# Largest scores in half blocks, layer statistics on ScalarE, and first and last groups with their own places in the order

## The chip, the cores and the metric

The kernel runs on one NeuronCore of a Trainium2 chip. The metric is the device time of one execution in microseconds (us), the median of several runs of the same program.

## The reference, cut to what matters

One decoder layer works on 64 sequences of 128 tokens with 512 channels. It has three sublayers, each with a layer norm before it and a residual around it:

```python
x = x + ssm(layernorm(x))            # in-projection, causal conv of 4, silu, selective scan
                                     # over 128 tokens with 16 states per channel, gate, out-projection
x = x + attn(layernorm(x), ctx)      # banded attention over the 512 *channels* of a sequence
x = x + moe(layernorm(x))            # 8 experts of width 16, the 2 best per token

# layernorm(x) = (x - mean) / sqrt(var + 1e-5), over the 512 channels of a token
# attn: the roles of tokens and channels are swapped, so there are 512 positions of 128 features,
#       8 heads of 16; position q sees the positions k with |q - k| <= 64
scores = einsum('bqhd,bkhd->bhqk', q, k) / sqrt(16)
scores = where(|q - k| <= 64, scores, most_negative)
attn   = softmax(scores)             # exp(s - max(s)) / sum
```

Two pieces of this are touched: the mean and the variance of each layer norm, and the largest score of each query, which the softmax subtracts.

## The kernel before, in words

The sequences are taken two at a time: 32 groups, each with 256 tokens (`TG`). The work of a group is written as generators ("strands"): `fetch`, `front` (layer norm, transposes, in-projection, conv), `silu0..3`, `project`, `rows_b`, `rows_c`, `dt0`, `dt1` (step sizes), `gate0..3`, `out_proj`, and then for each of the two sequences `attend` and `tail`, and at the end `experts`. The scan over the states is cut into 32 steps for each group (8 blocks of 128 channels, 4 quarters of the states), and each step has the parts `by_b` (GpSimd makes the input h), `decays` (ScalarE makes exp into PSUM), `scan` (VectorE, two halves), `by_c` (VectorE, or `by_c_far` on GpSimd for three steps of eight) and `summed` (TensorE).

The order of all of this is written out by hand and holds for all engines. `PLAN` gives every yield of a strand a place, in steps from the group's first scan step. `STEP` gives each part of a scan step its shift. All items of all groups are sorted by place (lines 910 to 931), and called in that order. So strands of up to five groups are interleaved: while group g is scanned (places 0 to 31), group g+1 goes through `front` to `dt`, group g-1 through `attend` and `tail` (35 to 61), and `experts` of a group comes at 63 to 78. Each engine then works through its own instructions strictly in that order, and waits on semaphores for the others. Since the places are the same for every group, the trace repeats itself from group to group.

Names and lines that matter:

- `moments` (429 to 436): for each of the two sequences, `bn_stats` over 512 channels and `bn_aggr`, on VectorE. It is called three times for each group: at the start of `front` (tile `xf`), after the out-projection (`xr`, called b) and at the start of `experts` (`xr`, called c). `inv_std` (438 to 447) turns the result into scale and bias on GpSimd, and `normalise` (449) applies them on ScalarE.
- `scores` (661 to 676) fills two PSUM tiles `ps_a` (tag "a", two banks each, two buffers in all). First four bf16 matmuls of the identity with the band mask (448 columns), then eight fp32 matmuls of 16 rows (one head at row 32r, four heads side by side), each for a block of 128 queries against 192 or 256 keys. `PAIRS` lists the blocks. `attend` calls it four times for the largest scores (tile `sq`), and VectorE reduces each of the two PSUM tiles with two `tensor_reduce` calls, one for each block (715 to 722). Later `scores` is called again with the roles of queries and keys swapped (tile `sk`), for the exponentials (line 746). That use is not touched.
- The largest scores go through a transposing matmul (`pm`), ScalarE (`nm`) and a small DMA into row 16 of `qT`, where the second scores take them in.
- `take_b` has one PSUM buffer, and serves in-projection, step sizes, transposes, projections of `tail` and `experts`.
- `th` (two buffers in SBUF) is the scratch of `silu`. `dtr`, `dur` (two buffers each) hold the rows of a scan block, `qT`, `kT`, `oT` have one buffer each.

Of the kernel before, what the change touches and what calls it, by code (L numbers as in the profile page):

```python
# [10 lines left out]
BF16 = mybir.dt.bfloat16  # L11
# [6 lines left out]
P = 128  # L18
H = 512
# [24 lines left out]


# [10 lines left out]
        -60.332,  # L56
    ),
    "front": (
        -54.904, -43.416, -41.272, -40.492, -39.654, -38.695, -38.685, -37.888, -36.879,
        -36.408, -36.032, -33.704, -33.145, -32.67, -32.66, -32.343, -31.799, -31.044, -30.174,  # L60
        -28.281, -27.454, -26.855, -26.832,
    ),
    "silu0": (
        -24.781, -24.46, -24.257,
    ),
    "silu1": (
        -29.838, -26.427, -25.073,
    ),
    "silu2": (
        -27.027, -26.806, -24.454,  # L70
    ),
    "silu3": (
        -22.5, -22.354, -21.641,
    ),
    "project": (
        -21.132, -21.099, -20.786, -19.777,
    ),
    "rows_b": (
        -11.803, -11.114, -2.288, -1.642,
    ),  # L80
    "rows_c": (
        -6.008, -5.135, -0.454, -0.226,
    ),
    "dt0": (
        -19.146, -19.123, -18.828, -18.586, -18.576, -18.517, -18.507, -18.497, -16.555,
        -16.496, -16.464, -16.226, -15.68, -14.582, -13.949, -11.966, -9.752,
    ),
    "dt1": (
        -8.54, -8.53, -7.168, -6.931, -4.396, -3.985, -3.344, -2.893, -2.009, -0.644, -0.166,
        1.263, 3.073, 6.784, 6.958, 7.293, 9.75,  # L90
    ),
    "gate0": (
        -5.443, 3.125, 3.277, 3.457,
    ),
    "gate1": (
        6.075, 6.704, 6.947, 6.957,
    ),
    "gate2": (
        11.935, 13.43, 13.746, 14.883,
    ),  # L100
    "gate3": (
        17.102, 18.411, 19.344, 19.54,
    ),
    "out_proj": (
        14.098, 15.108, 25.166, 27.955, 28.249, 28.897, 31.185, 31.344, 33.251, 34.471, 34.878,
        35.042,
    ),
    "attend0": (
        35.319, 35.465, 35.633, 36.089, 36.766, 37.24, 37.729, 37.739, 38.09, 38.1, 38.319,
        38.329, 38.606, 38.616, 38.847, 38.915, 38.925, 39.077, 39.333, 39.384, 39.646, 39.769,  # L110
        39.874, 40.107, 40.224, 40.234, 40.244, 40.509, 40.621, 41.595, 41.894, 42.165, 42.565,
        42.575, 42.887, 42.954, 42.964,
    ),
    "tail0": (
        41.092, 43.917, 43.927, 44.704, 45.578, 45.841, 45.851, 47.675, 48.362, 48.641, 49.437,
        49.792,
    ),
    "attend1": (
        43.598, 44.297, 44.545, 44.882, 44.892, 45.231, 45.409, 45.569, 45.741, 46.002, 46.012,
        46.644, 46.9, 46.991, 47.295, 47.744, 47.933, 47.943, 48.059, 48.685, 48.695, 49.273,  # L120
        49.283, 50.058, 50.791, 50.801, 51.134, 51.424, 51.549, 51.851, 51.861, 52.706, 52.72,
        53.308, 53.741, 53.751, 54.874,
    ),
    "tail1": (
        49.808, 55.232, 56.972, 57.846, 59.014, 59.685, 59.961, 60.274, 60.284, 60.387, 61.028,
        61.206,
    ),
    "experts": (
        62.814, 64.883, 65.122, 65.98, 66.07, 66.08, 66.253, 66.772, 67.628, 67.64, 69.657,
        69.884, 70.093, 70.31, 70.406, 71.21, 72.072, 72.112, 72.932, 73.648, 73.928, 78.062,  # L130
# [3 lines left out]
STEP = {  # L134
    "loads": (-3.6, 0, 0, 0, -3.754, 0, 0, 0),
    "by_b": (-0.407, -0.939, -0.855, -0.458, -0.757, -0.972, -1.605, -1.622),
    "decays.0": (-0.306, -0.611, -0.011, -0.125, -0.644, -0.63, -0.649, -0.336),
    "scan.0": (0, 0.29, 0.673, 0.224, -0.426, -0.43, -0.079, 0.045),
    "by_c.0": (0, 0.685, 0.811, 0, -0.425, -0.117, 0, 0.212),
    "decays.1": (0.032, -0.305, 0.297, 0.193, -0.488, -0.409, -0.309, -0.213),  # L140
# [854 lines left out]
```

## Time and profile before

| | |
|---|---|
| runs of the kernel | 5680.31, 5680.67, 5683.51 us (median 5680.67) |
| the profiled execution's own time | 5693.28 us |
| its span, first to last instruction | 5691.6 us |
| TensorE matmul busy | 4854.9 us (85%) |
| VectorE busy | 4729.5 us (83%) |
| GpSimd busy | 4562.8 us (80%) |
| ScalarE busy | 3701.2 us (65%) |
| first scan starts, last scan starts | 135.5 us, 5537.8 us |
| mean granted TensorE clock | 0.921 |

"Busy" is the time in which the engine has an instruction in work; matmuls are pipelined, and their ends are modelled. The lines of the page name the source line (L719 is line 719), the engine, the operation, and the tiles "out<-in" with partitions x elements. PE is TensorE, PEld its weight loads, DVE VectorE, ACT ScalarE, POOL GpSimd, SP the engine that issues the DMAs. A matmul of fp32 leaves two records in the trace, one of bf16 leaves one. The chain of waits follows the program back from its last instruction, at each step to what released it.

In the middle of the run the start of every 64th scan, one for each group, lies 170.1 us after the last one (mean over the groups 3 to 28). The first group takes 150.5 us.

### The profile page before, as it was taken

What the parts mean: (1) busy time and instruction counts of PE and PEld (TensorE: products, weight loads), DVE (VectorE), ACT (ScalarE), POOL (GpSimd) and SP (SyncE); (2) the same over time, 40 slices, a digit from 0 to 9 for tenths busy, and PEclk for the clock granted to TensorE, in tenths of its full rate; (3) what the DMA queues carried; (4) which work ended last, traced back from release to release, by engine and by line L of the source; (5) the groups of instructions that cost most, each with busy time, mean ns of one, the idle gap of its engine ahead of it and who ended that gap; (6) DMA issues with size and microseconds to landing.
All of it is one profiled execution on the core that took longest, in us unless ns stands there. A gap on an engine that the chain in (4) does not pass through costs nothing.

```text
span 5691.6 us, 91135 instructions
## 1 busy us (share of the span) xinstructions
PE 4854.9 (85%) x33348; PEld 2698.4 (47%) x33348; DVE 4729.5 (83%) x6896; ACT 3701.2 (65%) x7138; POOL 4562.8 (80%) x2818
## 2 busy tenths in 40 slices
PE   4689888889888889888889888889888888888886
PEld 3345445445445445545445445445444444444432
DVE  2788888888888888888888888888888888888882
ACT  2566767666767666667666667676666676666752
POOL 4888888888888788888888888888888888888860
PEclk7899999999999999999999999999999999999887
DMA  2333333333333333333333333333333333333320
GB/s 79 118 112 110 125 114 129 121 115 107 125 117 126 122 114 113 119 117 127 124 112 116 118 116 125 131 108 117 121 109 129 127 120 108 118 119 115 120 87 20
DMA packets 282192, 650.00 MB, mean 114 GB/s; under 512 B 48912, under 2 KB 116496, under 8 KB 281744
## 3 DMA queue, kind: packets, MB, share of 16 engines
q1 hardware_dynamic: 281744, 644.18, 33.3%
q8 instruction: 262, 4.29, 0.3%
q14 instruction: 186, 1.52, 0.1%
HBM read 557.04 MB, written 85.98 MB: 113 GB/s over the span
## 4 chain that ended last, share of the span: by engine, by line
PE 52%; DVE 19%; ACT 18%; issue 4%; DMA 4%; POOL 3%; SPq 0%; DVEq 0%; POOLq 0%; ACTq 0%
PE pin L463 9%; DVE mx L719 7%; ACT da L366 6%; PE yp L407 5%; PE pg L463 5%; PE sk L671 4%; PE po L644 4%; PE sq L671 3%; DVE hc L385 3%; PE pw L793 3%; ACT pe L746 3%; DVE u L512 3%; PE sk L665 3%; PE pa L753 2%; PE sq L665 2%
## 5 line engine op out<-in xcount | busy, mean ns | idle before, releaser
L354 POOL TENSOR_TENSOR h<-dur,brep 128x1024 f32<-128x1024 f32 x1024 | 2423.1, 2375 | 217.1 <-DVE da L385 171.2
L366 ACT ACTIVATE da<-dtr,acol 128x256 f32<-128x256 f32 x4096 | 1923.2, 476 | 837.7 <-DVE hc L385 398.6
L385 DVE TENSOR_TENSOR_SCAN da<-da,h 128x512 f32<-128x512 f32 x1280 | 1542.2, 1219 | 171.5 <-ACT da L366 135.2
L395 POOL TENSOR_TENSOR hc<-hc,crep 128x1024 f32<-128x1024 f32 x384 | 905.6, 2358 | 574.7 <-DVE hc L385 544.2
L385 DVE TENSOR_TENSOR_SCAN hc<-da,h 128x512 f32<-128x512 f32 x768 | 912.8, 1213 | 169.9 <-ACT da L366 83.3
L390 DVE TENSOR_TENSOR hc<-da,crep 128x512 f32<-128x512 f32 x1280 | 855.3, 685 | 59.2 <-PE yp L407 14.5
L407 PE MATMUL yp<-hc,sely 128*32 128x256 f32 x8192 | 754.5, 431 | 52.9 <-POOL hc L395 40.0
L719 DVE TENSOR_REDUCE mx<-sq 128x2 f32<-128x512 f32 (+1 forms) x1024 | 570.9, 614 | 175.7 <-PE sq L671 175.7
L746 ACT ACTIVATE pe<-sk 128x896 f32<-128x896 f32 x512 | 445.0, 915 | 137.9 <-PE sk L671 135.3
L463 PE MATMUL pin<-xnT,wi 128*128 128x256 f32 x2048 | 515.5, 408 | 21.4 <-DVE u L512 7.5
L463 PE MATMUL pg<-xnT,wi 128*128 128x256 f32 x2048 | 489.7, 393 | 8.1 <-DVE u L512 5.0
L644 PE MATMUL po<-wo,y 128*128 128x512 f32 x1024 | 470.2, 602 | 0.5 <-DVE y L415 0.5
L463 PEld LDWEIGHTS pin<-xnT,wi 128*128 128x128 f32 x2048 | 407.6, 204 | 129.5 <-ACT brep L566 23.7
L512 DVE SCALAR_TENSOR_TENSOR u<-pin,cw,u 128x254 f32<-128x254 f32 (+2 forms) x768 | 309.1, 471 | 164.5 <-ACT u L504 164.3
L463 PEld LDWEIGHTS pg<-xnT,wi 128*128 128x128 f32 x2048 | 388.2, 195 | 110.3 <-ACT dt L589 15.6
L665 PE MATMUL sq<-mask,identb 128*128 128x448 bf16 x1024 | 289.8, 384 | 159.2 <-DVE mx L719 154.8
L665 PEld LDWEIGHTS <-identb 128*128 128x128 bf16 x2048 | 162.0, 100 | 526.6 <-DVE mx L719 288.2
L407 PEld LDWEIGHTS yp<-hc,sely 128*32 128x32 f32 x8192 | 203.6, 114 | 404.6 <-issue 201.9
L671 PE MATMUL sk<-qT,kT 32*128 32x192 f32 (+1 forms) x4096 | 272.3, 381 | 45.6 <-DMA qT<-nm 45.6
L671 PE MATMUL sq<-kT,qT 16*128 16x192 f32 (+1 forms) x4096 | 300.6, 413 | 0.0
L644 PEld LDWEIGHTS po<-wo,y 128*128 128x128 f32 x1024 | 193.7, 192 | 222.4 <-issue 217.9
L665 PE MATMUL sk<-mask,identb 128*128 128x448 bf16 x1024 | 265.4, 373 | 28.6 <-ACT pe L746 21.6
(149 smaller groups left out, 6739.6 us busy)
## 6 DMA issues: line engine op xcount, KB each, us to landing
wi<-in_w_inproj SPq DMA_DIRECT2D x256, 512.0 KB
dtr<-dtd SPq DMA_DIRECT2D x256, 512.0 KB
dur<-dud SPq DMA_DIRECT2D x256, 512.0 KB
wo<-in_w_outproj SPq DMA_DIRECT2D x128, 512.0 KB
dtd<-dt SPq DMA_DIRECT2D x256, 128.0 KB
dud<-e SPq DMA_DIRECT2D x256, 128.0 KB
rc<-rd SPq DMA_DIRECT2D x256, 128.0 KB
xf<-in_x SPq DMA_DIRECT2D x64, 256.0 KB
```

Of the source, the lines that this page charges most:

```text
L354: nc.gpsimd.tensor_tensor(hs[k], dur[g, ib], brep[g, j // 2][:, j % 2, :].unsqueeze(1).to_broadcast([P, 4, TG]), ALU.mult,)
L366: nc.scalar.activation(das[k, half][:, s, :], dtr[g, ib][:, c, :], AF.Exp, scale=acol[:, col : col + 1])
L385: nc.vector.tensor_tensor_scan(flat(to), flat(d), flat(hs[k][:, own, :]), 0.0, ALU.mult, ALU.add)
L390: nc.vector.tensor_tensor(product(k)[:, 2 * half : 2 * half + 2, :], das.pop((k, half)), c_rows(k, 2), ALU.mult)
L395: nc.gpsimd.tensor_tensor(hcs[k], hcs[k], c_rows(k, 4), ALU.mult)
L407: nc.tensor.matmul(yps[g, ib][32 * c : 32 * c + 32, :], sely, h[:, c, :], start=False, stop=(j == NJ - 1), skip_group_check=True,)
L463: nc.tensor.matmul(ps[:, s * TG : (s + 1) * TG], w[:, s, k, :], flat3(xnT[g][:, k, :, :]), start=(k == 0), stop=(k == HC - 1),)
L644: nc.tensor.matmul(po[:, b, :], y[g, c][:, b * P : (b + 1) * P], w[:, c - c2, :], start=(c == 0), stop=(c == IC - 1),)
L665: nc.tensor.matmul(ps[r // 2][:, r % 2, :PAIR], identb, mask[:, i * EDGE : i * EDGE + PAIR], start=True, stop=False,)
L671: nc.tensor.matmul(ps[r // 2][:, r % 2, c0 : c0 + r1 - r0], left[32 * r : 32 * r + rows, s, blk * P : (blk + 1) * P], right[32 * r : 32 * ...
L719: nc.vector.tensor_reduce(mx[:, blk, h0 : h0 + 2], ps[rp][:, :, c0 : c0 + r1 - r0], AX.X, ALU.max,)
L746: nc.scalar.activation(t, ps[rp][:, :, :PAIR], AF.Exp, scale=0.25)
```

## The change

1. A new function `largest` takes the place of `scores` for the largest scores. It works in half blocks of 64 queries. Every half block sees exactly 192 keys (`WIN`), from `first_key`. Where `scores` had eight matmuls of 128 queries with 192 or 256 keys, `largest` has sixteen of 64 queries with 192 keys: four heads side by side in the rows, and two halves (queries 0 to 63 and 64 to 127 of a block) side by side in the columns. A new mask `maskq` of 3 x 192 columns is built at the start, and the mask matmuls have 384 columns. VectorE reduces each PSUM tile with one `tensor_reduce` of 768 elements, with four results for each partition, in place of two of 512 and 384.
2. `moments` goes to ScalarE: for each sequence one ACTIVATE Identity with scale -1/512 whose accumulator gives minus the mean, and one ACTIVATE Square with that as its bias, whose accumulator gives the sum of squares. Its scratch tile `sq` shares the tag `th`. `inv_std` scales the sum by 1/512. After the residual add of the out-projection a yield is added, so that `moments` b has its own place.
3. All places in `PLAN` and `STEP` are new. The first group has its own places for `front` to `dt`, the last group for `out_proj` to `experts`. In the last sequence of all, `qT` and `kT` lie in buffers of `dtr` and `oT` in one of `dur`.

The program has 4096 fp32 matmuls of 64 queries for these scores in place of 2048 of 128, 512 reduces for 1024, no `bn_stats` or `bn_aggr` (384 instructions less), and 384 more ACTIVATEs. The number of activation table loads is the same, 129, and the number of DMAs too. The orders on the engines have the same pieces between the same neighbours for most of a group. ScalarE has `moments` b behind the copy `xfT` of the first sequence and ahead of the copy `plv`, `moments` c behind the conv start `u` of the second in-projection, and `moments` a ahead of the relu of `pw`. For the first group, the two `pbrep` products come ahead of and behind `pts`, and the statistics of group 1 ahead of the step sizes of group 0. At the end, the 21 small VectorE operations of the experts of group 30 stand ahead of the reduces of group 31, and not among them.

The diff without the tables of places:

```diff
+WIN = 3 * LOCAL
 PLAN = {
...
+def first_key(q0):
+    return min(max(q0 - LOCAL, 0), H - WIN)
...
+    nc.gpsimd.memset(maskf[:, : 3 * WIN], 0.0)
+    for c, q0s in enumerate(((0, LOCAL), (P, P + LOCAL), (H - P, H - LOCAL))):
+        for q0 in q0s:
+            off = first_key(q0) - q0
+            m = maskf[q0 % P : q0 % P + LOCAL, c * WIN : (c + 1) * WIN]
+            select(m, ALU.is_ge, LOCAL + off, [[1, WIN]], -1, NEG)
+            select(m, ALU.is_ge, LOCAL - off, [[-1, WIN]], 1, NEG)
+    maskq = fixed([P, 3 * WIN], "maskq", dtype=BF16)
+    nc.vector.tensor_copy(maskq, maskf[:, : 3 * WIN])
...
     def moments(src, name):
-        mv = work([P, GB, 2], "mv", 3, f"mv_{name}")
-        st = [work([P, 6], "st", 4, f"st_{name}_{b}") for b in range(GB)]
-        for b in range(GB):
-            nc.vector.bn_stats(st[b], src[:, b, :])
-        for b in range(GB):
-            nc.vector.bn_aggr(mv[:, b, :], st[b])
+        mv = work([P, 2, GB], "mv", 3, f"mv_{name}")
+        sq = work([P, H], "th", 2, f"sq_{name}")
+        for b in range(GB):
+            nc.scalar.activation(
+                sq, src[:, b, :], AF.Identity, scale=-1.0 / H, accum_out=mv[:, 0, b : b + 1]
+            )
+        for b in range(GB):
+            nc.scalar.activation(
+                sq, src[:, b, :], AF.Square, bias=mv[:, 0, b : b + 1],
+                accum_out=mv[:, 1, b : b + 1],
+            )
         return mv
...
-        nc.gpsimd.tensor_scalar(rs[:, 0, :], mv[:, :, 1], EPS, None, ALU.add)
+        nc.gpsimd.tensor_scalar(rs[:, 0, :], mv[:, 1, :], 1.0 / H, EPS, ALU.mult, ALU.add)
...
         nc.vector.tensor_tensor(flat(t), flat(po), flat(t), ALU.add)
+        yield
         mv = moments(t, f"b{g}")
...
+    def largest(q, k, s, i, name):
+        ps = [take_a(f"{name}_{s}_{i}_{rp}") for rp in range(2)]
+        for r in range(4):
+            nc.tensor.matmul(
+                ps[r // 2][:, r % 2, : 2 * WIN], identb, maskq[:, i * WIN : (i + 2) * WIN],
+                start=True, stop=False, skip_group_check=True,
+            )
+        for half in range(4):
+            q0 = (4 * i + half) * LOCAL
+            k0 = first_key(q0)
+            for r in range(4):
+                nc.tensor.matmul(
+                    ps[r // 2][
+                        q0 % P : q0 % P + LOCAL, r % 2, half // 2 * WIN : (half // 2 + 1) * WIN
+                    ],
+                    q[32 * r : 32 * r + HD, s, q0 : q0 + LOCAL],
+                    k[32 * r : 32 * r + HD, s, k0 : k0 + WIN],
+                    start=False, stop=(half == 3), skip_group_check=True,
+                )
+        return ps
...
     def attend(g, b):
+        far = g == n_groups - 1 and b == 1
...
-                ps = scores(qT, kT, HD, s, i, f"sq_{n}")
+                ps = largest(qT, kT, s, i, f"sq_{n}")
                 for rp in range(2):
                     yield
-                    for blk, c0, r0, r1 in PAIRS[i]:
-                        h0 = 4 * s + 2 * rp
-                        nc.vector.tensor_reduce(
-                            mx[:, blk, h0 : h0 + 2], ps[rp][:, :, c0 : c0 + r1 - r0],
-                            AX.X, ALU.max,
-                        )
+                    h0 = 4 * s + 2 * rp
+                    nc.vector.tensor_reduce(
+                        mx[:, 2 * i : 2 * i + 2, h0 : h0 + 2].rearrange("p k h -> p h k"),
+                        ps[rp][:, :, : 2 * WIN].rearrange("p h (k j) -> p h k j", j=WIN),
+                        AX.X, ALU.max,
+                    )
...
+    def own(g, name):
+        if g == 0 and name.startswith(("front", "silu", "project", "rows", "dt")):
+            return "_first"
+        if g == n_groups - 1 and name.startswith(("out_proj", "attend", "tail", "experts")):
+            return "_last"
+        return ""
...
-            for p in PLAN[name]:
+            for p in PLAN[name + own(g, name)]:
```

## The prediction, made before the run

> **What bounds the kernel now.** I read the page first, then the repeating stretch in the middle, then the waits of each engine, and last the single operations that the change touches.
>
> ```profile
> PE 4854.9 (85%) x33348; PEld 2698.4 (47%) x33348; DVE 4729.5 (83%) x6896; ACT 3701.2 (65%) x7138; POOL 4562.8 (80%) x2818
> PE 52%; DVE 19%; ACT 18%; issue 4%; DMA 4%; POOL 3%; SPq 0%; DVEq 0%; POOLq 0%; ACTq 0%
> ```
>
> Three engines are nearly equally full. The chain runs mostly over PE, a fifth each over DVE and ACT. Busy time by windows of one group each:
>
> ```profile
> 2007.00:2177.00 170.00, 149.59 (x1045) 82.62 (x1043) 147.65 (x216) 115.63 (x225) 142.11 (x87) 0.93 0.35 119
> sum 510.00, PE 447.64 PEld 248.68 DVE 441.50 ACT 345.50 POOL 424.90; mean PE 149.21 PEld 82.89 DVE 147.17 ACT 115.17 POOL 141.63
> ```
>
> A group takes 170.1 us (spacing of the first scans), and PE, DVE and POOL work 149, 147 and 142 of it. Each stands still for 21 to 28 us, so nobody is a clean bound. The waits of the whole run say who waits for whom:
>
> ```profile
> POOL hc L395 <- DVE hc L385: 544.2, 233, 11.7
> ACT da L366 <- DVE hc L385: 398.6, 196, 9.2
> DVE mx L719 <- PE sq L671: 175.7, 131, 12.9
> PE sq L665 <- DVE mx L719: 154.8, 227, 2.3
> DVE da L385 <- ACT da L366: 135.2, 210, 1.7
> ```
>
> POOL and ACT wait for DVE. PE waits for DVE at the largest scores, and DVE for PE there. That place, `sq` and `mx`, is where the change cuts. In the chain of the stretch 2007 to 2177 it looks like this, and nearly all eight score tiles of a group lie on it:
>
> ```profile
> 2076.22 0.76 PE sq L665 x4
> 2076.98 0.98 PE sq L671 x16
> 2077.98 2.22 DVE mx L719 x4
> ```
>
> **Part 1, the reduces.** Groups by shape:
>
> ```profile
> L719 DVE TENSOR_REDUCE mx<-sq 128x2 f32<-128x512 f32 x512 | 348.7, 681 | 94.7 <-PE sq L671 94.7
> L719 DVE TENSOR_REDUCE mx<-sq 128x2 f32<-128x384 f32 x512 | 280.5, 548 | 81.0 <-PE sq L671 81.0
> L433 DVE BATCH_NORM_STATS2 st_b<-xr 128x6 f32<-128x512 f32 x64 | 41.2, 686 | 1.1
> L435 DVE BATCH_NORM_AGGREGATE mv_b<-st_b 128x2 f32<-128x6 f32 x64 | 9.6, 173 | 0.0
> L549 ACT ACTIVATE th<-u 128x512 f32<-128x512 f32 x128 | 79.7, 623 | 4.6 <-POOL u L553 2.6 <-DVE u L512 2.0
> L450 ACT ACTIVATE xf<-xf,rs_a 128x512 f32<-128x512 f32 x64 | 48.1, 799 | 19.4 <-POOL rs_a L444 19.4
> ```
>
> 128 more elements cost 681 - 548 = 133 ns, so 1.04 ns each above 149 ns. One reduce of 768 should take 149 + 768 x 1.04 = 948 ns. A group has 16 x 681 + 16 x 548 = 19.7 us of reduces now, and 16 x 948 = 15.2 us after: 4.5 us less DVE work. On the chain a run of four takes 2.14 to 2.23 us (overlapping by 0.09 at each seam), and two would take 2 x 0.948 - 0.09 = 1.80, so 0.38 less. From 1000 to 5082 us the chain has L719 on it with 7.3%, 12.4 us of a group or 5.7 such runs. That gives **-2.1 us**.
>
> **Part 2, the score matmuls.** Mask matmuls follow each other by 189 ns for 448 columns, so 162 for 384. On the chain they have 3.7 us of a group, and a seventh of that is **-0.5 us**. The fp32 part isn't in the trace in its new form. Now four heads run side by side in the rows, in four passes one after the other (two for 192 keys at 162 ns, two for 256 at 216, the first 0.27 because it loads its weights in the open): 0.27 + 0.16 + 0.22 + 0.22 = 0.86 us. After, there are eight passes of 162 ns for each head. If the two column halves ran fully side by side it would be four passes, 0.27 + 3 x 0.16 = 0.75 us. If they ran one after the other, eight, 1.40 us. If an instruction only has to wait for its own half, the passes overlap like a chain of five: 0.27 + 4 x 0.16 = 0.92. I take 0.92, for this reason. The Trainium skill ("TensorE: Matmul & The Clock Gate", section "Part 3: Packing small matmuls — row/col tiling") says that a weight load overlaps running matmuls only when it goes to other rows of the array. By that rule the halves, which share their rows, queue up, with weight loads in the open too: 8 x (0.16 + 0.13), where 0.13 is between the 106 ns load of 32 columns and the 185 of 128. That is 2.3 us, 12 us more for a group. But this trace has four column tiles that share all rows:
>
> ```profile
> 2077.88 0.64 PE L407 MATMUL yp<-hc,sely 128*32 128x256 f32 x8
> ```
>
> Eight records of 256 columns in 0.64 us, where alone each takes 216 ns: they do overlap, weight loads included (these start 7 ns apart). So the row decides against the rule, and PE's load stays about where it is: (0.92 - 0.86 - 4 x 0.027) x 8 = -0.4 us, from -1.7 to +3.5 by the rows, +11 by the rule. On the chain: **0**.
>
> **Part 3, the statistics.** 6 x 0.68 + 6 x 0.173 = 5.1 us of DVE work go. They are hardly on the chain, but scans queue behind them. Outside the reduces, DVE's 127 us a group have 19 on the chain, 15%: **-0.8 us**. ACT gets two ACTIVATEs without a pointer operand (like L549, 0.62) and two with one (between 0.62 and 0.80), three times a group. With 0.09 overlap and a short wait for its own mean, that is 2.5 us each time, 7.5 a group. The accumulator's price is not in the trace: at least nothing (7 us a group), at most a second small instruction for each (12 x 0.22 us, L846), without overlaps 12 us. I take 7.5, by the row it is nearest to. The skill's "ScalarE: Activation LUTs" (section "Rules for kernel authors") says to leave adds and multiplies to VectorE; as a sum over both engines it is right here (7.5 for 5.1 us), but ACT is 68% full and DVE 87%. What is behind these ACTIVATEs on ACT are `decays`, and DVE's scans wait for those. By the order, `moments` b stands where DVE has two scans and two products ahead (3.8 us), c where it has two scans and six conv operations (4.8 us), a ahead of the relu of `pw`. All are longer than 2.5 us, so they mostly hide: **+0.6 us**. If that cover were gone all 7.5 would show. The extra latency of b and c (2.5 against 1.7) goes into strands with places to spare. POOL keeps its operations, SP its DMAs, and table loads stay at 129.
>
> **Part 4, the places.** In the middle the order has the same pieces between the same neighbours. I give the new places nothing; they may be worth 2 us either way.
>
> Sum for a group: -2.1 - 0.5 - 0.8 + 0.6 = -2.8 us; 31 spacings: -87 us. **The ends.** Before the first scan lie 135.5 us. Group 0's step sizes get two products, two copies and the statistics of group 1 ahead of them, but the first scan waits on ACT for the conv start of group 1 (132.07), itself behind a weight DMA and two in-projections, that is kept. I put +2. Building `maskq` costs POOL 0.6 + 12 x 0.36 = 4.9 us where it is idle for 35.6 us. After the last scan lie 153.8 us: seven runs of reduces, -2.7; statistics b and c, +2.2; the 21 small operations of the experts, which stood between two runs of reduces for 4.0 us, now run while PE makes q and k, -4. The buffers for the last `qT`, `kT`, `oT` free little: the chain there is one of data. Ends together -3. So 5693.3 - 87 - 3 = 5603 for the profiled execution; it lay 12.6 us above the median of 5680.7, so **5591, I say 5590**.
>
> **The rivals.**
> (a) DVE paces everything. For: most waits of POOL and ACT end on it. Against: half of the chain is PE's own work. Then the 9.6 us that DVE loses come back nearly whole, 8 a group: 5681 - 31 x 8 = 5430. Chance 0.12.
> (b) PE is the bound: its 149 us stay, the shorter reduces only turn PE's waits for `mx` into waits for something else (`pt` for ACT's step sizes has 229 us already), and ACT's extra work eats the rest. Also what would follow if an accumulator cost much. 5680, within 11 us. Chance 0.10.
> (c) Slower: the column halves of `largest` do not overlap. Place: between mask and reduce, on the chain. Price: 0.54 - 0.11 = 0.43 us x 8 = +3.4 us a group with hidden weight loads, against the -2.3 of the reduces, statistics and ScalarE: 5680 + 31 x 1.2 = 5717; with weight loads in the open, 5980. I put 5730, nearer the first, since loads overlap in every row here. It decides from 1.15 us for the sixteen matmuls, where its extra eats those 2.3. The loss would also come if all of `moments` lay open, +7.5 - 0.6 a group, 5804. Chance 0.25 together.
> The likeliest (d), DVE's savings on the chain and half hidden otherwise: 0.53.
>
> **How the numbers follow.** Two tenths of a per cent, 11 us, is about what a measurement can tell from no change. (d) alone runs from 5540 to 5645: the places at 2 us a group either way make 62 us, the score matmuls between -0.8 and 0 on the chain 25. To leave no more than 2 in 10 out, the range takes in (b), half of (c), and the upper part of (a): 5500 to 5725. Faster: 0.53 + 0.12 = 0.65; same 0.10; slower 0.25.
>
> **What would show it.** Right: the spacing of first scans near 167.3; reduces near 950 ns; a sixteen-matmul block near 0.92 us; PE's 149 unchanged, DVE near 138, ACT near 123. Wrong: score blocks of 1.4 us or more; ACT rows with accumulator above 0.9 us; DVE's wait for `da` (135 us in the run) doubled; PE's waits grown by what `mx` gave back.

## The result, and the profile after

The changed kernel takes 5699.83 us (median of 7 runs, 5693.75 to 5711.18), the kernel before 5681.42 us beside it (7 runs). The ratio is 1.0031, 95% interval 1.0020 to 1.0043: slower by a third of a per cent, inside the stated range, but slower where faster was forecast. The profiled execution of the changed kernel took 5698.44 us, its span is 5696.3 us. The mean clock granted to TensorE was 0.904 to 0.909 in the seven runs; in the timed runs of the kernel before it lay between 0.915 and 0.924.

The shares of the span and the chain of waits:

```profile
PE 4828.3 (85%) x37444; PEld 2725.5 (48%) x37444; DVE 4544.7 (80%) x6001; ACT 3977.4 (70%) x7906; POOL 4577.8 (80%) x2831
PE 49%; ACT 20%; DVE 17%; issue 4%; DMA 4%; POOL 3%; SPq 1%; DVEq 0%; ACTq 0%; POOLq 0%
```

Busy time in the windows of the middle (columns as before: PE, PEld, DVE, ACT, POOL, clock, DMA):

```profile
2007.00:2177.00 170.00, 148.29 (x1170) 84.13 (x1169) 141.01 (x188) 123.37 (x247) 141.60 (x87) 0.92 0.35 118
sum 510.00, PE 444.89 PEld 252.45 DVE 423.40 ACT 370.03 POOL 424.74; mean PE 148.30 PEld 84.15 DVE 141.13 ACT 123.34 POOL 141.58
```

DVE lost 6.0 us a group of busy time (8.8 us as a sum of durations), ACT gained 8.2, PE lost 0.9, at a clock of 0.92 where it was 0.93. Yet the spacing of the first scans (groups 3 to 28) is 170.4 us, where it was 170.1: DVE is relieved, and the period doesn't move. The rest lies at the start: the first scan begins at 138.4 us, 2.9 later; after the last scan comes 153.2 us, 0.6 less.

The waits of the whole run:

```profile
DVE hc L467 <- ACT da L448: 196.4, 151, 3.1
...
DVE da L467 <- ACT da L448: 119.3, 168, 2.4
...
DVE mx L834 <- PE sq L780: 80.4, 63, 5.3
```

DVE waits 95 us less for the scores. Its waits for the decays (`da`) went from 219 to 316 us, and it has waits that it did not have before, shown below. Single operations, by shape:

```profile
L834 DVE TENSOR_REDUCE mx<-sq 128x4 f32<-128x768 f32 x512 | 464.3, 948 | 80.8 <-PE sq L780 80.4
L780 PE MATMUL sq<-kT,qT 16*64 16x192 f32 x8192 | 274.4, 383 | 0.0
L520 ACT ACTIVATE sq_b<-xr,mv_b 128x512 f32<-128x512 f32 x64 | 46.2, 722 | 2.1
L516 ACT ACTIVATE sq_b<-xr 128x512 f32<-128x512 f32 x64 | 40.4, 632 | 3.4 <-DVE xr L740 2.4
L516 ACT ACTIVATION_READ_ACCUMULATOR sq_b<-xr 128x1 f32 x64 | 12.2, 190 | 0.0
```

The reduce takes the 948 ns that were worked out. The score matmuls are as cheap as taken where the clock is full, and take 1.7 times as long where it is halved (shown under part 2 below). Each accumulator costs an instruction of its own, which the program does not name.

### The profile page after: what moved, and what is told of

The parts are those of the page before. It is cut to its first block, busy times and chain, and to the rows that moved or that the text cites. A ratio compares the mean times of both kernels' runs of the same rounds, so it can differ in the third digit from the quotient of the medians.

```text
span 5696.3 us, 99361 instructions
## 1 busy us (share of the span) xinstructions
PE 4828.3 (85%) x37444; PEld 2725.5 (48%) x37444; DVE 4544.7 (80%) x6001; ACT 3977.4 (70%) x7906; POOL 4577.8 (80%) x2831
## 4 chain that ended last, share of the span: by engine, by line
PE 49%; ACT 20%; DVE 17%; issue 4%; DMA 4%; POOL 3%; SPq 1%; DVEq 0%; ACTq 0%; POOLq 0%
PE pin L551 8%; ACT da L448 6%; PE po L732 6%; PE yp L489 5%; ACT pe L866 5%; DVE mx L834 4%; PE sk L760 4%; PE pg L551 4%; DVE da L467 3%; PE pw L913 3%; DVE hc L467 3%; PE sk L754 2%; PE sq L780 2%; PE pa L873 2%; PE pqk L799 2%
## 5 line engine op out<-in xcount | busy, mean ns | idle before, releaser
L472 DVE TENSOR_TENSOR hc<-da,crep 128x512 f32<-128x512 f32 x1280 | 869.8, 688 | 75.3 <-PE yp L489 19.9
L489 PE MATMUL yp<-hc,sely 128*32 128x256 f32 x8192 | 737.8, 420 | 83.0 <-POOL hc L477 65.4
L834 DVE TENSOR_REDUCE mx<-sq 128x4 f32<-128x768 f32 x512 | 464.3, 948 | 80.8 <-PE sq L780 80.4
L551 PE MATMUL pin<-xnT,wi 128*128 128x256 f32 x2048 | 495.5, 397 | 31.6 <-DVE xr L924 12.8
L551 PEld LDWEIGHTS pin<-xnT,wi 128*128 128x128 f32 x2048 | 395.0, 198 | 137.4 <-ACT crep L654 36.0
L772 PE MATMUL sq<-maskq,identb 128*128 128x384 bf16 x1024 | 274.3, 377 | 128.8 <-DVE mx L834 121.9
L754 PE MATMUL sk<-mask,identb 128*128 128x448 bf16 x1024 | 288.9, 383 | 71.1 <-ACT pe L866 34.8
L780 PE MATMUL sq<-kT,qT 16*64 16x192 f32 x8192 | 274.4, 383 | 0.0
L760 PEld LDWEIGHTS sk<-qT,kT 32*128 32x128 f32 x4096 | 189.7, 200 | 156.7 <-DMA qT<-nm 81.1
```

The costliest lines, as they stand in the source:

```text
L472: nc.vector.tensor_tensor(product(k)[:, 2 * half : 2 * half + 2, :], das.pop((k, half)), c_rows(k, 2), ALU.mult)
L489: nc.tensor.matmul(yps[g, ib][32 * c : 32 * c + 32, :], sely, h[:, c, :], start=False, stop=(j == NJ - 1), skip_group_check=True,)
L551: nc.tensor.matmul(ps[:, s * TG : (s + 1) * TG], w[:, s, k, :], flat3(xnT[g][:, k, :, :]), start=(k == 0), stop=(k == HC - 1),)
L754: nc.tensor.matmul(ps[r // 2][:, r % 2, :PAIR], identb, mask[:, i * EDGE : i * EDGE + PAIR], start=True, stop=False,)
L760: nc.tensor.matmul(ps[r // 2][:, r % 2, c0 : c0 + r1 - r0], left[32 * r : 32 * r + rows, s, blk * P : (blk + 1) * P], right[32 * r : 32 * ...
L834: nc.vector.tensor_reduce(mx[:, 2 * i : 2 * i + 2, h0 : h0 + 2].rearrange("p k h -> p h k"), ps[rp][:, :, : 2 * WIN].rearrange("p h (k j) ...
```

## The experiments

Two theories stood against each other. Theory 1: the statistics cost far more on ScalarE than the 0.6 us taken for them. Theory 2: the new places cost, which were given nothing. (In the expectations below, S is theory 1 and P is theory 2; W says that what is saved turns into waits wherever it is saved.) The three parts of the change can be separated, so the first six experiments fill a table of operations by places. "Old places" means the tables `PLAN` and `STEP` of the kernel before (and no yield ahead of `moments` b). All were timed beside the kernel before, whose median was 5682.58 to 5695.57 us from one timing to the next, so ratios are compared. "A group" is the spacing of the first scans, as above.

**1. The largest scores alone, old places.**

```diff
-            nc.scalar.activation(
-                sq, src[:, b, :], AF.Identity, scale=-1.0 / H, accum_out=mv[:, 0, b : b + 1]
-            )
...
+            nc.vector.bn_stats(st[b], src[:, b, :])
+        for b in range(GB):
+            nc.vector.bn_aggr(mv[:, b, :], st[b])
...
-    "loads": (-2.237, 0, 0, 0, -4.054, 0, 0, 0),
+    "loads": (-3.6, 0, 0, 0, -3.754, 0, 0, 0),
...
```

> The kernel before with the half-block largest scores alone; statistics stay on VectorE, all places are the old ones. Theory P (the operations give what the prediction summed, and the new places lose it again): 2.6 us less a group, 5681 - 31 x 2.6 = 5600 us. Theory W (the reduces' saving turns into waits wherever it is put, because the engines wait for each other in a ring): 5681 within 20 us. Theory S (the statistics on ScalarE lose what the reduces gain): 5600 us, as P.

Measured 5578.18 us, ratio 0.9795 (0.9779 to 0.9812), spacing 166.6 us. Parts 1 and 2 of the prediction, the reduces and the score matmuls, bring 2 %, more than the whole forecast.

**2. The statistics alone, old places** (`scores` and `PAIRS` reduces for the largest scores as before).

```diff
-                ps = largest(qT, kT, s, i, f"sq_{n}")
+                ps = scores(qT, kT, HD, s, i, f"sq_{n}")
```

> The kernel before with the statistics on ScalarE alone, old places. P: the statistics are nearly free, +0.6 - 0.8 us a group, 5681 within 25 us. W: 5681 within 25 us too, since ScalarE has idle time. S: each of the three pieces of 3.3 us (two ACTIVATEs of 0.63, two of 0.72, four reads of the accumulator of 0.19, less overlap) holds up the decays behind it and with them the scans, about 3 us a group, 5775 us.

Measured 5883.29 us, 1.0332 (1.0306 to 1.0358). This is 6 us a group (176.1 against 170.1), twice what theory 1 expected.

**3. Both, old places.** The changed kernel with the tables of before:

```diff
-        yield
         mv = moments(t, f"b{g}")
...
-    "loads": (-2.237, 0, 0, 0, -4.054, 0, 0, 0),
+    "loads": (-3.6, 0, 0, 0, -3.754, 0, 0, 0),
...
```

> The kernel before with both operations changed and all places old. P: 5590 us, the prediction's own sum, since it gave the new places nothing. W: 5681 within 25 us. S: 5600 + 95 = 5695 us, about what the changed kernel takes.

Measured 5786.98 us, 1.0162 (1.0144 to 1.0181), spacing 173.3.

**4. The new places alone**: the changed kernel with the scores and the statistics of before.

```diff
-                ps = largest(qT, kT, s, i, f"sq_{n}")
+                ps = scores(qT, kT, HD, s, i, f"sq_{n}")
...
+            nc.vector.bn_stats(st[b], src[:, b, :])
...
```

> The changed kernel with the old operations put back (scores of 128 queries with two reduces, statistics on VectorE): only the places are new. P: the new places alone cost what the operations gain, 5681 + 110 = 5790 us. W: 5681 to 5720 us. S: the new places are neutral, 5681 within 30 us.

Measured 5814.65 us, 1.0209 (1.0192 to 1.0226), spacing 174.1.

**5. The largest scores with the new places**, statistics on VectorE (the second edit of experiment 4 alone).

> The changed kernel with the statistics back on VectorE; half-block scores and new places stay. So far: half-block scores alone 0.9795, statistics on ScalarE alone 1.0332, both 1.0162, new places alone 1.0209. Theory S (the statistics on ScalarE are the loss in any order): about as much faster than the changed kernel as in the old order, 5700 - 200 = 5500 us. Theory O (order and operations belong together: the new places were made for statistics on ScalarE, and there they cost little): 5690 to 5720 us, the sum of the new places' own loss (+119) and the reduces' gain (-117).

Measured 5698.43 us, 1.0030 (1.0019 to 1.0040), spacing 170.7.

**6. The statistics with the new places**, scores as before (the first edit of experiment 4 alone).

> The changed kernel with the old scores and two reduces; statistics on ScalarE and new places stay. S: new places +119 and statistics +188 add up, 5990 us. O: the statistics cost little or nothing in the order that has room for them, 5815 us or less (the changed kernel 5700 and the reduces' 117).

Measured 5749.30 us, 1.0117 (1.0104 to 1.0131). The table, as ratios to the kernel before:

| | old places | new places |
|---|---|---|
| scores of before, statistics on VectorE | 1 | 1.0209 |
| largest, statistics on VectorE | 0.9795 | 1.0030 |
| scores of before, statistics on ScalarE | 1.0332 | 1.0117 |
| both | 1.0162 | 1.0031 (the change) |

Both theories hold, and they are tied to each other. Read down: `largest` gains in every pair (2.05, 1.70, 1.79 and 0.86 %). The statistics cost 3.3 and 3.7 % at the old places, and gain 0.9 % or nothing at the new. Read across: the new places cost 2.1 and 2.4 % where the statistics are on VectorE, and give back 2.2 and 1.3 % where they are on ScalarE. The new order fits the moved statistics, and costs elsewhere about as much as `largest` brings. How much of each of these differences goes with the granted clock is looked at behind experiment 17.

**7. The ends.** The changed kernel without the own places of the first and the last group, and without the other buffers of the last sequence:

```diff
-            for p in PLAN[name + own(g, name)]:
+            for p in PLAN[name]:
...
-        far = g == n_groups - 1 and b == 1
+        far = False
```

> The changed kernel without places of their own for the first and last group: all groups use the general places, and the last sequence the usual buffers. If the own places help at the ends: up to 20 us slower than the changed kernel, 5720 us. The spans of the ends (135.5 and 153.8 us before, 138.4 and 153.2 us after) say that they do little: 5700 us within 8 us.

Measured 5698.27 us, 1.0028 (1.0017 to 1.0039): the ends make no difference that can be told.

**8. Occupancy or latency.** Experiment 1, and ScalarE makes its passes too, into tiles that nobody reads; the statistics used are VectorE's. So ScalarE's time is added, nothing waits for its results, and VectorE keeps its work.

```diff
         for b in range(GB):
             nc.vector.bn_aggr(mv[:, b, :], st[b])
+        dv = work([P, 2, GB], "dv", 3, f"dv_{name}")
+        sq = work([P, H], "th", 2, f"sq_{name}")
+        for b in range(GB):
+            nc.scalar.activation(
+                sq, src[:, b, :], AF.Identity, scale=-1.0 / H, accum_out=dv[:, 0, b : b + 1]
+            )
...
         return mv
```

> The half-block scores with old places (5578 us) and statistics on VectorE, whose values are used. In addition ScalarE makes the same twelve passes with accumulators at the same places of its queue, and nobody reads their results. So ScalarE is as full as with the statistics on it, but no chain hangs on it. If it is ScalarE's occupancy that holds up decays and scans: as slow as both operations together, 5787 us, or a little over, since VectorE keeps its 5.1 us a group (5800 to 5850). If it is the chain of accumulator, GpSimd and normalise, with GpSimd's queue held at the scale (127 us of waits in the run with statistics alone): near 5578 us, at most 5620.

Measured 5755.15 us, 1.0127 (1.0113 to 1.0140). Of the 3.7 % between experiments 1 and 3, 3.3 come from ScalarE's time alone. The later result matters little, and so does what VectorE is spared.

**9. One place changed.** From the trace I worked out how long ScalarE has nothing in work between the starts of scan step k and k+1 of a group (experiment 1, mean of twelve groups). It is 51 us in all, but 0.2 us in each of the steps 2 and 3, where b stands at the old places, 0.6 and 0.2 in the steps 8 and 9, where a stands, 6.0 in step 31, where c stands, and 10.3 in step 6. In experiment 3 just the steps 1 to 3 are longer (by 3.0 us together) and 8 and 9 (by 3.5), and 31 is not. So a was moved from step 9 to step 6, in experiment 3:

```diff
     "front": (
-        -54.904, -43.416, -41.272, -40.492, -39.654, -38.695, -38.685, -37.888, -36.879,
+        -57.6, -43.416, -41.272, -40.492, -39.654, -38.695, -38.685, -37.888, -36.879,
```

> Both operations with the old places (5787 us), and one number changed: the statistics a, 3.3 us on ScalarE, move from step 9 of the scan to step 6. In the run with half-block scores alone ScalarE stands still for 10.3 us of step 6, and for 0.2 us of step 9. Theory I (a piece costs in full where ScalarE has no idle time in that step, and nothing where it has): the 3.5 us a group that the run with both operations lost around step 9 come back, 5787 - 31 x 3.5 = 5680 us. If the mere load of ScalarE counts, 5787 within 15 us.

Measured 5691.07 us, 1.0012 (1.0004 to 1.0020). One number takes off 1.5 %. Step 9 is back from 7.75 to 4.95 us, and step 6 grows no longer (13.96 and 13.94 us, means of 25 groups), while ScalarE's idle time in it falls from 10.6 to 7.6.

**10. a (moved) and c on ScalarE, b on VectorE**, largest scores, old places. The edit of experiment 9, and

```diff
     def moments(src, name):
+        return (moments_s if name[0] in "ac" else moments_d)(src, name)
```

> Half-block scores, old places, statistics a (moved to step 6) and c (step 31, 6.0 us of idle ScalarE) on ScalarE, b back on VectorE. I: nothing lost against half-block scores alone (5578 us), and the 3.4 us of VectorE work a group that go save up to 2 us a group: 5520 to 5578, say 5560 us. If the load of ScalarE counts: two thirds of the 177 us that twelve passes with unread results cost, 5690 us.

Measured 5606.66 us, 0.9857 (0.9844 to 0.9871). A miss: this was to beat experiment 1, and is 0.5 to 0.6 % slower. VectorE is spared 3.4 us a group and nothing comes of it.

**11 and 12. Which table costs?** Experiment 5 (largest, new places) with the old `STEP`, and experiment 1 (largest, old places) with the new `STEP`.

```diff
-    "by_b": (-0.434, 0.126, -0.462, -0.28, -0.571, -1.445, -1.504, -1.889),
+    "by_b": (-0.407, -0.939, -0.855, -0.458, -0.757, -0.972, -1.605, -1.622),
...
```

The diff is that of experiment 11; 12 has it the other way round.

> Half-block scores and statistics on VectorE with the new places of the strands, but the old shifts of the scan's parts. The same operations take 5578 us in the old order and 5698 in the new one. If the strands carry that loss: 5690 us. If the shifts of the scan do: 5590 us. If both only fit together: over 5700 us.

> Half-block scores and statistics on VectorE with the old places of the strands and the new shifts of the scan's parts. If the strands carry the loss of the new order: 5590 us. If the shifts do: 5690 us. If both only fit together: over 5700 us.

Measured 6026.71 us, 1.0594 (1.0579 to 1.0608), and 6027.33 us, 1.0600 (1.0585 to 1.0614). Inconclusive: each half of the new order is far worse with the old other half. The tables belong together, so swapping one of them does not tell which holds the cost.

**13 to 16. One piece at a time**, all on experiment 1: b alone on ScalarE, c alone, a alone at its old place, a alone at the earlier place. (`moments_s` is the changed function, `moments_d` that of before.)

```diff
     def moments(src, name):
+        return (moments_s if name[0] in "b" else moments_d)(src, name)
```

> The largest scores in half blocks at the old places (5578 us), with statistics b alone on ScalarE. Theory A (a piece costs what ScalarE's idle time in its step doesn't cover; at the steps 2 and 3 ScalarE has 0.2 us idle each): +3.0 us a group, 31 x 3.0 = 93, so 5670 us. Theory B (the three pieces together overfill ScalarE, and one alone is absorbed by its 51 us of idle time in a group): within 12 us of 5578.

> The same with statistics c alone on ScalarE, at step 31, where ScalarE has 6.0 us idle. Theory A: +0.2 us a group, 5584 us. Theory B: within 12 us of 5578 too. If c is what made the version with a (moved) and c 28 us slower, it is about 5600.

> The same with statistics a alone on ScalarE, at its old place (step 9, where ScalarE has 0.2 us idle, and 0.6 in the step before). Theory A: +3.5 us a group, 5687 us. Theory B: within 12 us of 5578.

> The same with statistics a alone on ScalarE, at the earlier place (step 6, 10.3 us idle). Theory A: 0 to +0.5 us a group, 5578 to 5594 us, so about 96 us below the run with a at its old place. Theory B: no difference between the two places of a.

Measured: b 5691.38 us, 1.0012 (1.0003 to 1.0021); c 5595.71, 0.9844 (0.9830 to 0.9857); a 5654.34, 0.9946 (0.9933 to 0.9958); a moved 5585.11, 0.9824 (0.9811 to 0.9838). Against 0.9795 that is +2.2, +0.5, +1.5 and +0.3 %. The pieces add up: 2.2 + 0.5 + 1.5 = 4.2 % for the 3.7 that they cost together. One piece alone is not absorbed by 51 us of idle time elsewhere in the group; it decides where it stands. In size the account by steps was off both ways, if the ratios are turned into us a group: b cost 4.0, not 3.0, a 2.8 and not 3.5 (a gives 0.8 us back in the steps 6 and 8, b loses 1.2 more there), c 0.9 and not 0.2. For b and c most of this goes with the clock, as shown behind experiment 17.

Piece b in experiment 13. ScalarE's timeline (start, time, what):

```profile
2169.27 0.99 ACT L385 ACTIVATE da<-dtr,acol 128x256 f32<-128x256 f32 x2
2170.20 0.61 ACT L473 ACTIVATE sq_b<-xr 128x512 f32<-128x512 f32 x1
...
2173.26 0.80 ACT L501 ACTIVATE xn<-xr,rs_c 128x512 f32<-128x512 f32 x1
2173.97 0.97 ACT L385 ACTIVATE da<-dtr,acol 128x256 f32<-128x256 f32 x2
```

VectorE's beside it:

```profile
2170.30 1.23 DVE L404 TENSOR_TENSOR_SCAN da<-da,h 128x512 f32<-128x512 f32 x1 [0.87 <-ACT da L385]
2171.57 0.69 DVE L409 TENSOR_TENSOR hc<-da,crep 128x512 f32<-128x512 f32 x1
2175.02 1.22 DVE L404 TENSOR_TENSOR_SCAN hc<-da,h 128x512 f32<-128x512 f32 x1 [2.77 <-ACT da L385]
```

The piece takes 3.1 us (2170.20 to 2173.26), between the decays of one scan and those of the next. VectorE has one scan and one product left, 1.9 us, and then stands for 2.8 us. In experiment 1 the same scans follow each other without it:

```profile
2131.89 1.22 DVE L404 TENSOR_TENSOR_SCAN da<-da,h 128x512 f32<-128x512 f32 x1
2133.14 0.69 DVE L409 TENSOR_TENSOR hc<-da,crep 128x512 f32<-128x512 f32 x1
2133.75 1.21 DVE L404 TENSOR_TENSOR_SCAN hc<-da,h 128x512 f32<-128x512 f32 x1
```

At the new places the cover is there. In the changed kernel ScalarE has b behind the decays of two more scans:

```profile
2163.67 1.89 ACT L448 ACTIVATE da<-dtr,acol 128x256 f32<-128x256 f32 x4
2167.02 0.58 ACT L942 COPY xfT<-ptc 128x512 f32<-128x512 f32 x1 [1.47 <-PE ptc L544]
2167.51 0.63 ACT L516 ACTIVATE sq_b<-xr 128x512 f32<-128x512 f32 x1
...
2170.74 1.90 ACT L448 ACTIVATE da<-dtr,acol 128x256 f32<-128x256 f32 x4
```

and VectorE works through them:

```profile
2169.19 1.22 DVE L467 TENSOR_TENSOR_SCAN da<-da,h 128x512 f32<-128x512 f32 x1
...
2171.82 2.34 DVE L467 TENSOR_TENSOR_SCAN hc<-da,h 128x512 f32<-128x512 f32 x2 [0.68 <-POOL rs_b L530]
2176.21 0.69 DVE L712 SCALAR_TENSOR_TENSOR gt<-gt,pg 128x512 f32<-128x512 f32 x1 [2.05 <-ACT gt L710]
```

ScalarE's idle time at this place is 3.4 us in experiment 5, which has the new order and nothing to fill it, and 0.1 us in the changed kernel. The new order holds a gap open for the piece. The last line shows a wait that came with that order: VectorE stands for the tanh of the gate. In the stretch from 1000 to 5082 us, by group, experiment 5 has these waits of VectorE that experiment 1 lacks: 2.3 us for that tanh, 1.7 for the products of the step sizes on GpSimd, 1.0 for their exp, 0.9 for a row of sums from a DMA, and 3.5 more for decays ahead of the `hc` scans; its wait for the score matmuls falls from 4.8 to 0.3.

**17. One such wait taken out**, in the changed kernel. The product stands ahead of a scan whose decays are ready:

```diff
     "gate0": (
-        -5.691, 2.931, 3.333, 3.625,
+        -5.691, 2.931, 3.333, 4.0,
```

> The changed kernel with one number of its places changed: the product of the first gate on VectorE, at 3.625 just ahead of the first scan of step 4, goes to 4.0, behind that scan. In the changed kernel VectorE stands still for 2.04 us a group ahead of that product, while the scan behind it has had its decays for 0.5 us by then. Theory A (the new order costs by waits like this one, each where it stands): the scan starts up to 1.2 us earlier in each group, 1 us x 31 = 31 us, so about 5669 us, 5655 to 5685. Theory B (the period is set elsewhere, by TensorE or GpSimd, and VectorE only waits in another place): within 10 us of the changed kernel's 5700.

Measured 5653.94 us, 0.9947 (0.9933 to 0.9961), 0.84 % below the changed kernel, 1.4 us a group (169.0 for 170.4). VectorE's timeline at this place:

```profile
2157.34 2.34 DVE L467 TENSOR_TENSOR_SCAN hc<-da,h 128x512 f32<-128x512 f32 x2 [0.68 <-POOL rs_b L530]
2161.56 1.23 DVE L467 TENSOR_TENSOR_SCAN da<-da,h 128x512 f32<-128x512 f32 x1 [1.88 <-POOL h L436]
...
2163.50 0.68 DVE L712 SCALAR_TENSOR_TENSOR gt<-gt,pg 128x512 f32<-128x512 f32 x1
```

The wait for the gate is gone, and one of 1.9 us for GpSimd's `h` has come. The scan starts 0.8 us earlier behind the last one (4.22 us for 4.99), but nothing is left of that one scan later: the steps 3 and 4 together take 9.76 us for 9.75. What becomes shorter is mainly step 6 (13.65 to 12.68), step 8 (by 0.4) and step 14 (by 0.3). So the time came out near theory A's, and not in the way of theory A.

**What the clock has in it** (from the traces of the runs above). The clock records of a trace grant TensorE the full clock or half of it. The stretches at half clock are 3.41 us long, or a multiple of that. One group of the changed kernel can differ from the next in this, although both run the same instructions in the same order. Its groups 20 and 21 (counted from 0), then two groups of experiment 17 (us of the group, busy times, third from the end the mean granted clock; 0.92 over 170.8 us stands for 27.3 us at half clock, 0.94 over 168.1 us for 20.5):

```profile
3522.92:3693.72 170.80, 148.89 (x1174) 84.40 (x1170) 141.75 (x188) 124.06 (x248) 142.27 (x87) 0.92 0.35 119
3693.72:3861.86 168.14, 145.85 (x1174) 82.68 (x1170) 141.76 (x189) 124.28 (x248) 142.24 (x87) 0.94 0.35 120
1805.21:1973.48 168.27, 146.00 (x1174) 82.59 (x1170) 141.80 (x189) 124.23 (x248) 142.33 (x87) 0.94 0.36 120
1973.48:2143.13 169.65, 147.62 (x1174) 83.30 (x1170) 141.88 (x189) 124.13 (x248) 142.31 (x87) 0.93 0.35 119
```

Between the first two only TensorE's time (PE, PEld) differs by more than 0.3 us, PE's by 3.0. The changed kernel (groups 3 to 27) has 27.3 us at half clock and 170.7 us in 21 groups, 23.9 and 169.6 in two, 20.5 and 168.2 in two. Experiment 17 has 23.9 and 169.6 in thirteen groups, 20.5 and 168.3 in twelve. With the same time at half clock the two kernels take the same. Step 6 shows it alone, again in the groups 20 and 21 of the changed kernel:

```profile
3555.27:3569.11 13.84, 11.12 (x139) 6.68 (x138) 11.87 (x31) 4.16 (x10) 3.35 (x2) 0.87 0.01 1
3726.08:3738.76 12.68, 9.67 (x134) 5.95 (x133) 12.10 (x31) 3.97 (x9) 3.36 (x2) 0.97 0.00 1
```

The second, without the product moved, is as short as step 6 of experiment 17. So experiment 17 does not show that the wait for the gate cost anything; its gain goes with the clock. The runs over the groups 3 to 27 (the experiments 3 and 8 have no group with 20.5 us at half clock):

| | mean of a group, us | of it at half clock | groups with 20.5 us at half clock: their mean (how many) |
|---|---|---|---|
| the kernel before | 170.1 | 21.4 | 170.1 (13) |
| 1, largest, old places | 166.6 | 17.7 | 167.3 (15) |
| 2, statistics, old places | 176.1 | 24.2 | 175.1 (5) |
| 4, new places alone | 174.1 | 26.6 | 172.9 (4) |
| 5, largest, new places | 170.7 | 20.5 | 170.7 (25) |
| 6, statistics, new places | 171.5 | 24.2 | 170.9 (7) |
| the changed kernel | 170.4 | 26.5 | 168.2 (2) |
| 7, no places of their own for the ends | 170.3 | 26.2 | 168.0 (3) |
| 17, product moved | 169.0 | 22.3 | 168.3 (12) |
| 13, b alone | 170.6 | 23.1 | 170.2 (5) |
| 14, c alone | 167.3 | 19.7 | 167.3 (13) |
| 15, a alone | 169.0 | 20.5 | 169.0 (23) |
| 16, a moved | 166.9 | 19.0 | 167.2 (18) |
| 10, a moved and c | 167.4 | 20.8 | 167.3 (22) |

The last column is no measurement at a fixed clock: where the half-clock stretches fall counts too, and groups of one run with the same time at half clock can lie 1.2 us apart (in the kernel before). But its larger differences are clear. `largest` brings 2.8 us and the rest of its 3.5 goes with the clock. The new places cost 2.7 to 3.4 us, and not 4. In the new order the statistics save 2.5 us, and 6 us more at half clock take nearly all of it away. At places where ScalarE is idle (experiments 10, 14 and 16) the statistics then cost nothing, b costs 2.9 us, as its steps say (3.0), and a at its old place 1.7, less than its step says. The costs in the steps 1 to 3 and 9 themselves are not the clock's: in experiments 1, 3 and 15 none of these steps has more than 0.3 us at half clock in the mean.

Over the runs of the kernel before, whose clock moves between 0.915 and 0.924, 1 % less clock goes with 0.5 % more time. If that held from kernel to kernel, the lower clock of the changed kernel (1.6 %) would be worth 0.8 %, or 46 us. This is an estimate; with it the change would be about half a per cent faster than the kernel before, and not slower. What makes TensorE get the full clock more or less often was not tested. The fastest version of all stays experiment 1, with nothing but `largest` in it.

## Why the prediction was wrong, step by step

**Part 1, the reduces: right.** 948 ns came out as 948. Parts 1 and 2 were put at -2.6 us a group; alone at the old places they give -3.5 us (170.1 to 166.6), and -2.8 between groups with the same time at half clock. The steps that shrink are those with the largest scores in them (5, 6, 8 and 13 to 16).

**Part 2, the score matmuls: right at the full clock.** The sixteen matmuls were taken as 0.92 us. The chain of the changed kernel has

```profile
2021.21 0.89 PE sq L780 x32
2077.04 1.56 PE sq L780 x32
```

The first block runs at the full clock, the second at half. (168 blocks lie wholly at the full clock, with a median of 0.91 us, and 62 wholly at half, with 1.58. Before, it was 1.04 and 1.88.) So the prediction's sign of being wrong, "score blocks of 1.4 us or more", is seen, but the column halves are not its cause. The eight matmuls of before were put at 0.86 us, where the line that the prediction shows has 0.98. Over the run a block has TensorE busy for 274.4 / 256 = 1.07 us, before 300.6 / 256 = 1.17. The rule of the Trainium skill ("TensorE: Matmul & The Clock Gate", section "Part 3: Packing small matmuls — row/col tiling"), by which weights for the same rows wait, would have made 2.3 us of it. The measurement speaks against it for column halves of fp32, and rival (c) falls with its main mechanism. (Its threshold of 1.15 us left out the 0.11 us that the mask matmuls give back; with them it is 1.26.)

**Part 3, the statistics: the number right in the new order by luck, and wrong as a property of the change.** One size was off: 2.5 us a piece left out the accumulator reads, four of 0.19 us, and it is 3.1 (ScalarE's load rose by 8.2 us a group, for 7.5). In the new order the forecast was -0.2 us a group, and experiment 5 and the changed kernel differ by -0.3. But that is two things that cancel: about -2.5 at the same time at half clock, and 6 us more at half clock. Both kernels stand at 170.7 us in most of their groups, which is 50.0 of the 3.41 us stretches of the clock. At the old places "they mostly hide" is wrong, and the bound "all 7.5 would show" was nearer: 6.7 us with `largest`, 6.0 without. There VectorE's saved work was worth nothing: where it was spared the same work at a covered place it waited instead (experiments 10, 14 and 16).

**Part 4, the places, and the clock: the steps that failed.** "In the middle the order has the same pieces between the same neighbours. I give the new places nothing; they may be worth 2 us either way." They cost 4.0 us a group with the operations of before (174.1 for 170.1), and 4.1 with `largest` (170.7 for 166.6); at the same time at half clock it is 2.7 and 3.4, still outside the 2 us. I read the cover of the statistics from the new order, and took the order itself as free: two halves of one account, of which I booked one. Neighbours that stay the same say which instruction waits behind which, and not for how long. The gate's product had the same neighbours on VectorE, and stood for 2.0 us instead of nothing.

The second term at nothing was the granted clock. It stands in the prediction's own windows (0.93), but no part and no rival has a price for it. In the changed kernel it fell to 0.92, with 26.5 us of a group at half clock for 21.4, and this is worth about 2.2 us a group (168.2 to 170.4).

So the sum a group, at the same time at half clock, is: -2.8 from `largest` (put at -2.6), +3.4 from the places (put at 0), -2.5 from the statistics (put at -0.2), together about -2 for the -2.8 that were forecast; and about +2.2 that go with the clock. In the ratios as measured it is -2.05 % from `largest`, +3.67 % from the statistics at the old places, -1.31 % from the places that cover them; together +0.31 %. The other way round: places +2.1 %, `largest` -1.8, statistics 0.0.

**The ends**, put at -3 us: the run without their own places is the same, and the spans show +2.9 ahead of the first scan and -0.6 behind the last. The statistics cost more there than the +2 and +2.2 put for them: between experiment 5 and the changed kernel the first scan comes 9.0 us later, and 10.4 us more lie behind the last.

**The rivals.** (a) falls: DVE lost 6 us of busy time and the period kept its length. (b) named the outcome, the gain eaten elsewhere and the time unchanged within 20 us, but not its way: PE's load stays, but the 2 % of experiment 1 (2.8 us a group at the same time at half clock) show that it was no bound. No rival named the clock. Of (c), the mechanism of the score matmuls is refuted. Its side remark, that all of `moments` could lie open, is what the old places show.

**What stays open.** Which waits make up the new order's cost is not settled. One of them was tried (experiment 17), and taking it out gave nothing at the same time at half clock. The others are in the trace, but were not moved. That the gaps for the statistics cost by themselves is argued from ScalarE's idle time in experiment 5, and no run shows it apart. Why the changed kernel has more time at half clock, and whether another order would get it back, no run shows: none held the clock.

## What to carry to other kernels

On an engine that works strictly in order, a moved operation costs what the idle time of that engine at that very place doesn't cover, however idle it is elsewhere: make a table of idle time by step, for each engine, before believing that something hides. When a change brings a new order along, price the order as a part of its own. Try the parts alone: here one of three parts was worth 2 %, and the two others cost it. And before a difference of a per cent is put down to a wait, compare groups at the same granted clock: one run of one program has groups of 168 and of 171 us.

## What the runs showed of the hardware that was not expected

- An ACTIVATE with an accumulator leaves a second instruction in the trace, ACTIVATION_READ_ACCUMULATOR, of 186 to 191 ns. With it one pass over 512 columns takes 0.75 to 0.85 us from start to start, where the row alone says 0.63 to 0.72.
- Two column halves of 64 cost TensorE nothing against one of 128, although there are twice as many fp32 matmuls and weight loads: 1.07 us of busy time for sixteen, 1.17 for eight of more columns. The 32 weight loads of a block took 151 ns each in the mean; a block of 0.89 us has no room for them in the open.
- VectorE could be given 3.4 us less work in a group without any gain (experiment 10). Taking out a wait of 2.0 us left the scans one step later where they were (experiment 17).
- TensorE's clock was granted in full or by half, in stretches of 3.41 us and its multiples. In experiment 5 every group from 3 to 27 takes 170.7 us, 50.0 such stretches, and 21 of the 25 groups of the changed kernel do too, although ScalarE and VectorE do different work in them. So equal times of two kernels can hide a difference of 2 us in the work of a group. That the period is held there by the clock is not shown.
